# Moving key counts from a routing stage to the experts, with smaller last routing chunks and the first expert's rows read in pieces

## The chip, the cores and the metric

The kernel runs on one core of one Trainium2 chip. The metric is device time in microseconds of one execution; a median of several executions is compared. All data is float32, and everything from the input `x` to the output is one launch.

The core has five engines, each with a queue of its own that is worked off in order: TensorE (PE in the profile; its weight loads are PEld), VectorE (DVE), ScalarE (ACT), GpSimd (POOL) and SyncE (SP). Transfers are issued from SP's, ACT's or POOL's queue and run on 16 DMA engines.

## The reference, cut to what matters

The reference is a network of two layers on `x` of shape (2, 1024, 256), so 2048 tokens of 256 values. Each layer is an adapter, an attention, another adapter and a feed-forward part:

```python
x = x + L0_attn(L0_cond(x))      # adapter, then an RWKV-like recurrence
x = x + L0_ffn(L0_cond2(x))      # two-layer adapter (256 -> 1024 -> 256), then 8 experts, top 2
x = x + L1_attn(L1_cond(x))      # dense or sparse attention, then local attention
x = x + L1_ffn(L1_cond2(x))
```

The change lies in the second line and at the start of the third. The experts' part takes the two largest of eight gate logits of each token, keeps at most 512 tokens an expert in the order of arrival (first all first choices, then all second choices), and adds up the weighted results:

```python
for k in range(TOP_K):
    oh = jax.nn.one_hot(idx[:, k], E, dtype=jnp.int32)
    pos = jnp.cumsum(oh, axis=0) - 1 + counts[None, :]
    keep = (oh == 1) & (pos < CAPACITY)
    counts = counts + jnp.sum(keep.astype(jnp.int32), axis=0)
    combine = combine + w[:, k][:, None] * keep.astype(jnp.float32)
for e in range(E):
    h = jax.nn.gelu(xf @ W1[e] + b1[e])
    ye = h @ W2[e] + b2[e]
    out = out + combine[:, e][:, None].astype(xf.dtype) * ye
```

The sparse form of `L1_cond` lets each of 1024 queries attend to 32 listed keys, whose numbers lie between 0 and 255 and can occur more than once. A softmax over a list with repeats is a softmax over all keys, with the logarithm of each key's count added to its score. The kernel computes it so.

## The kernel before, in words

Activations are kept transposed, as tiles of 128 channels by tokens, in blocks of 128 tokens. There are 16 blocks.

**cond2 and routing.** `cond2_0` works through the chunks of `C2CK` (line 607): three of four blocks, one of three, one of one. For each chunk TensorE multiplies by the first weights into `ph` (L629), ScalarE applies Gelu (L632), TensorE multiplies by the second weights into `po` (L638), once for each half `c` of the 256 channels, and VectorE adds the bias into `c2` (L645). Then `choose(ch)` computes the gate logits `pl` (L723), copies them to `L` (L727), transposes the tokens (L657) into rows `ct` (ScalarE, L729), and finds the two largest logits by a chain of small dependent VectorE operations (L735 to L745). `place(ch)` turns the choices `oh` into running counts by matmuls into `pc` (L758, L762), into slots (L767 to L778, the last being `si`), and scatters the rows into the DRAM table `xs` by indirect DMAs from POOL's queue (L781), two for each block. `place` of a chunk is issued one chunk later; the last two come at the end. `finish` computes the weights of the combination and the number of first choices of each expert.

**Experts.** `moe` loops over eight experts. SP loads the expert's 512 rows by first choice (`xe`) and by second choice (`more`), 544 KB each (L919). VectorE merges them (L921), and computes the rows to which the results go (`row`, L927 to L931). TensorE transposes (L936), ScalarE copies (`xt`, L937), TensorE multiplies into `ph` (L942), ScalarE applies Gelu into `h` (L945, two buffers), TensorE multiplies into `po` (L950, two buffers), VectorE adds the bias (`ye`, L953), POOL scatters to `ys` (L954). Weights of the expert after next are loaded by SP (L892, L894). Each expert is followed in the program by `count_keys`, which for one block of 128 queries compares the 256 key numbers `iok` with each of the 32 listed keys and adds up: 1 operation (L879) and 31 steps (L881) that depend on each other, then a mask for zero counts, a maximum with 1, a logarithm on ScalarE and a sum (L883 to L886). The result is `lc`.

**After the experts.** `combine` loads the results from `ys` by SP's and ACT's queues (L974), weights and adds them (L978, L979), transposes and adds into `x` (L981, L984). Then come the projections of `L1_cond` (L1046 and on) and its attention, whose first operation on the scores reads `lc` (L1164).

**What sets the order.** The program is written in the order above, but the instructions of each engine are ordered at compile time by a scheduler that fills an engine with later work when earlier work is not ready. Waits follow from the tiles that an instruction reads, writes or takes over. So `count_keys`, which depends only on small inputs loaded by `load_counts` (L860, L862) ahead of cond2, stands in VectorE's queue between the operations of cond2, far ahead of its place in the program. Tiles come from pools on the left or right side of the on-chip memory; a tile that takes over another's space waits for that tile's last user.

Of the kernel before, what the change touches and what calls it, by code (L numbers as in the profile page):

```python
# [9 lines left out]
F32 = mybir.dt.float32  # L10
I32 = mybir.dt.int32
U8 = mybir.dt.uint8
AF = mybir.ActivationFunctionType
# [5 lines left out]
P = 128  # L19
# [584 lines left out]

C2CK = [(0, 4), (4, 4), (8, 4), (12, 3), (15, 1)]


def cond2_0(k, x, o, choose, place):  # L610


    nc, tc = k.nc, k.tc
    with (
        tiles(tc, name="c2s", bufs=2) as sp,
        tiles(tc, name="c2p", bufs=3, space=PSUM) as pp,
        tiles(tc, name="c2q", bufs=2, space=PSUM) as qp,
    ):

        end = len(C2CK) - 1  # L620
        for ch, (b0, nb) in enumerate(C2CK):
            b = b0 * P // S
            n = nb * P
            ts = slice(b0 * P, b0 * P + n)
            h = sp.tile([P, 8, CK], F32, name="h")
            for m in range(8):
                ph = pp.tile([P, CK], F32, name="ph")
                for c in range(2):
                    nc.tensor.matmul(  # L629
                        ph[:, 0:n], lhsT=k.c2w1[:, c, m * P : (m + 1) * P], rhs=x[:, c, ts], start=c == 0, stop=c == 1  # L630
                    )
                nc.scalar.activation(h[:, m, 0:n], ph[:, 0:n], AF.Gelu, bias=k.vec("c2b1", m))  # L632
            if 0 < ch < end:
                place(ch - 1)
            for c in range(2):
                po = qp.tile([P, CK], F32, name="po")
                for m in range(8):
                    nc.tensor.matmul(  # L638
                        po[:, 0:n],
                        lhsT=k.c2w2[b][:, m, c * P : (c + 1) * P],  # L640
                        rhs=h[:, m, 0:n],
                        start=m == 0,
                        stop=m == 7,
                    )
                nc.vector.tensor_scalar_add(o[:, c, ts], po[:, 0:n], k.c2b2[b][:, c : c + 1])  # L645
            if ch == end:
                place(ch - 1)
            choose(ch)
        place(end)

# [200 lines left out]
            nc.vector.tensor_mul(k.cw[:, kk, :], val[kk], self.kept[:, :, kk])  # L851


def load_counts(k, pool):

    nc, ins = k.nc, k.ins
    k.idx = pool.tile([P, 8, 32], F32, name="idx")
    with tiles(k.tc, name="ldc", bufs=1) as lp:
        ii = lp.tile([P, 8, 32], I32, name="ii")
        nc.sync.dma_start(out=ii, in_=ins["idx"].rearrange("(q p) j -> p q j", p=P))  # L860
        mm = lp.tile([P, 8, 32], U8, name="mm")
        nc.sync.dma_start(out=mm, in_=ins["idxm"].rearrange("(q p) j -> p q j", p=P))  # L862
        mf = lp.tile([P, 8, 32], F32, name="mf")
        nc.vector.tensor_copy(mf, mm)
        nc.vector.tensor_copy(k.idx, ii)

        nc.vector.scalar_tensor_tensor(k.idx, k.idx, 1.0, mf, ALU.add, ALU.mult)
        nc.vector.tensor_scalar_add(k.idx, k.idx, -1.0)
    k.lc = pool.tile([P, 8, NEAR], F32, name="lc")
    k.iok = pool.tile([P, S], F32, name="iok")  # L870
    nc.gpsimd.iota(k.iok, pattern=[[1, S]], base=0, channel_multiplier=0, allow_small_or_imprecise_dtypes=True)


def count_keys(k, sp, n, qb):


    nc = k.nc
    key = k.iok[:, 0 : n.shape[-1]]
    nc.vector.tensor_scalar(n, key, k.idx[:, qb, 0:1], None, ALU.is_equal)  # L879
    for j in range(1, 32):  # L880
        nc.vector.scalar_tensor_tensor(n, key, k.idx[:, qb, j : j + 1], n, ALU.is_equal, ALU.add)  # L881
    none = sp.tile([P, n.shape[-1]], F32, name="none")
    nc.vector.tensor_scalar(none, n, 0.0, -BIG, ALU.is_equal, ALU.mult)  # L883
    nc.vector.tensor_scalar_max(n, n, 1.0)
    nc.scalar.activation(n, n, AF.Ln)
    nc.vector.tensor_add(n, n, none)  # L886


def load_expert(k, wp, e):
# [8 lines left out]
def moe(k, xs, ys, wp, loaded):  # L898


    nc, tc, ins = k.nc, k.tc, k.ins
    with (
        tiles(tc, name="mos", bufs=2) as sp,
        tiles(tc, name="moc", bufs=1) as cp,
        tiles(tc, name="mop", bufs=2, space=PSUM) as pp,
    ):
        b2 = cp.tile([P, E * C], F32, name="b2")
        nc.sync.dma_start(out=b2, in_=ins["mb2"].to_broadcast([P, E * C]))
        rows = dram_disjoint_views(ys[:], E * 4)

        own = cp.tile([P, E, 4], F32, name="own")
        nc.gpsimd.iota(
            own, pattern=[[CAP, E], [P, 4]], base=2 * T, channel_multiplier=1, allow_small_or_imprecise_dtypes=True
        )
        for e in range(E):
            w1, w2 = loaded[e]
            xe, more = (sp.tile([P, 4, ROW], F32, name=n) for n in ("xe", "more"))
            for t, r0 in ((xe, e * CAP), (more, NSLOT + e * CAP)):
                nc.sync.dma_start(out=t, in_=xs[r0 : r0 + CAP, :].rearrange("(j p) f -> p j f", p=P))  # L919
            for j in range(4):  # L920
                nc.vector.scalar_tensor_tensor(  # L921
                    xe[:, j, :], more[:, j, :], k.more[:, e, j : j + 1], xe[:, j, :], ALU.mult, ALU.add
                )

            no = xe[:, :, C]
            empty = sp.tile([P, 4], F32, name="empty")
            nc.vector.scalar_tensor_tensor(empty, no, 0.0, own[:, e], ALU.is_equal, ALU.mult)  # L927
            to = sp.tile([P, 4], F32, name="to")
            nc.vector.scalar_tensor_tensor(to, k.more[:, e], float(T), no, ALU.mult, ALU.add)
            row = sp.tile([P, 4], I32, name="row")  # L930
            nc.vector.scalar_tensor_tensor(row, to, -1.0, empty, ALU.add, ALU.add)  # L931
            xt = sp.tile([P, 2, CAP], F32, name="xt")
            for c in range(2):
                pt = pp.tile([P, CAP], F32, name="pt")
                for j in range(4):
                    nc.tensor.transpose(pt[:, j * P : (j + 1) * P], xe[:, j, c * P : (c + 1) * P], k.ident)  # L936
                nc.scalar.copy(xt[:, c, :], pt)  # L937
            h = sp.tile([P, 8, CAP], F32, name="h")
            for m in range(8):
                ph = pp.tile([P, CAP], F32, name="ph")  # L940
                for c in range(2):
                    nc.tensor.matmul(  # L942
                        ph, lhsT=w1[:, c, m * P : (m + 1) * P], rhs=xt[:, c, :], start=c == 0, stop=c == 1
                    )
                nc.scalar.activation(h[:, m, :], ph, AF.Gelu_apprx_tanh, bias=k.vec("mb1", e * 8 + m))  # L945
            ye = sp.tile([P, 4, C], F32, name="ye")
            for j in range(4):
                po = pp.tile([P, C], F32, name="po")
                for m in range(8):
                    nc.tensor.matmul(  # L950
                        po, lhsT=h[:, m, j * P : (j + 1) * P], rhs=w2[:, m, :], start=m == 0, stop=m == 7
                    )
                nc.vector.tensor_add(ye[:, j, :], po, b2[:, e * C : (e + 1) * C])  # L953
                nc.gpsimd.indirect_dma_start(  # L954
                    out=rows[e * 4 + j],
                    out_offset=bass.IndirectOffsetOnAxis(ap=row[:, j : j + 1], axis=0),
                    in_=ye[:, j, :],
                    in_offset=None,
                )
            if e + 2 < E:  # L960
                loaded.append(load_expert(k, wp, e + 2))
            count_keys(k, cp, k.lc[:, e, :], e)


def combine(k, x, ys):
# [20 lines left out]

def load_cond1(k, pool):
    nc, ins = k.nc, k.ins
    k.w1c = pool.tile([P, NW1C], F32, name="w1c")

    k.bk = pool.tile([P, 4], F32, name="bk")
# [276 lines left out]
def cond1_heads(k, b, qT, kT, v, aT, sp, pp, tp):  # L1268
# [6 lines left out]
    def scores(it):  # L1275
        qb, h0 = it["at"]
        if h0 == 0:
            mk8 = sp.tile([P, S], U8, name="mk8")
            nc.sync.dma_start(out=mk8, in_=ins["mask"][qb * P : (qb + 1) * P, :])
            mk = sp.tile([P, S], F32, name="mk", bufs=1)  # L1280
            nc.vector.tensor_scalar_add(mk, mk8, -1.0)
            t = state["bias", qb] = sp.tile([P, S], F32, name="bias")
            count_keys(k, sp, t, qb)
            nc.vector.tensor_scalar_mul(t, t, k.sel[:, b : b + 1])
            nc.vector.scalar_tensor_tensor(t, mk, k.coef[:, b : b + 1], t, ALU.mult, ALU.add)
        ps = [pp.tile([P, S], F32, name=f"ps{i}", bufs=1) for i in range(2)]
# [416 lines left out]
def program(ctx: ExitStack, tc: tile.TileContext, ins, out):  # L1703
# [40 lines left out]
    with tiles(tc, name="c", bufs=1) as cp, tiles(tc, name="w3k", bufs=1, side="right") as kp:  # L1744
        c2 = cp.tile([P, 2, T], F32, name="c2")
        with tiles(tc, name="cnt", bufs=1) as np_:
            with tiles(tc, name="mor", bufs=1, side="right") as rp:
                with tiles(tc, name="mow", bufs=2, side="right") as ep:
                    with tiles(tc, name="mort", bufs=1, side="right") as rt:
                        with (  # L1750
# [1 line left out]
                            tiles(tc, name="rtp", bufs=1, space=PSUM) as pp,  # L1752
                        ):
                            load_cond2_0(k, wp)
                            load_counts(k, np_)
                            load_cond1(k, np_)
                            loaded = [load_expert(k, ep, e) for e in range(2)]
                            route = Route(k, c2, xs, rp, rt, pp, pp)
# [121 lines left out]
```

## Time and profile before

| what | us |
|---|---|
| median of 3 runs | 1566.27 (1561.85 to 1575.56) |
| profiled execution | 1573.28 |
| its span, first to last instruction | 1571.6 |
| PE busy | 1453.8 (93%) |
| DVE busy | 876.0 (56%) |
| ACT busy | 686.1 (44%) |
| POOL busy | 186.6 (12%) |
| key count steps L881, 248 of them | 103.7 on DVE, between 302.9 and 438.4 |
| cond2 and routing on PE | 300.1 to 426.4 |
| experts on PE | 445.4 to 680 |

A line of the costliest groups gives line, engine, operation, output and inputs with shapes and count, then the busy time and the mean duration in ns, then the idle time of the engine ahead of them with what ended it. A line of the timeline gives the start, the duration, the engine, the line of the kernel and the operation, with the idle time of the engine ahead of it in brackets. The "queue" lines (SPq) are issues of transfers. The clock column is the TensorE clock that was granted, as a share of full speed. A float32 matmul shows as two records, so 16 records make one `po` tile of an expert.

### The profile page before, as it was taken

The page shows a single profiled execution, that of the slowest core. Times are in us where ns is not written, and L with a number is a line of the kernel's source. Part 1 is how long each engine was busy: PE and PEld are TensorE (multiplying, and loading weights), DVE is VectorE, ACT ScalarE, POOL GpSimd, SP SyncE. Part 2 cuts the span into 40 slices and gives each one's busy share as a digit, 9 for nine tenths or more (in the row PEclk, how much of TensorE's full clock was granted, in tenths as well). Part 3 has the DMA queues.
Part 4 walks back from the last instruction along what each step waited for, and adds up shares of the span by engine and source line. Part 5 has one row for each costly group of instructions (what it writes and reads, how often), then busy time and mean ns, then how long its engine had stood idle before and what let it go on. Part 6 is the DMA issues. An engine that isn't in the chain of part 4 may idle for free. (4 is left out here: it accounts for less than half of the span.)

```text
span 1571.6 us, 27458 instructions
## 1 busy us (share of the span) xinstructions
PE 1453.8 (93%) x10842; PEld 994.2 (63%) x10842; DVE 876.0 (56%) x2791; ACT 686.1 (44%) x1675; POOL 186.6 (12%) x167
## 2 busy tenths in 40 slices
PE   5998779999869999979999989999999999999897
PEld 2445768544646676655666634778886478888765
DVE  3544663599931111055888711788782167878454
ACT  2433013333421212204988821667574265656543
POOL 1532430014411011010000010000000000000021
PEclk8899678999979999987999999999999999999999
DMA  9500003401153333030000020000000000000001
GB/s 301 176 1 2 3 3 112 161 4 40 53 162 132 124 115 115 14 120 1 2 2 2 2 82 0 1 2 2 1 2 1 0 1 2 2 1 2 1 19 36
DMA packets 42631, 70.79 MB, mean 45 GB/s; under 512 B 7040, under 2 KB 35712, under 8 KB 39424
## 3 DMA queue, kind: packets, MB, share of 16 engines
q1 hardware_dynamic: 36224, 56.11, 10.7%
q0 software_dynamic: 3072, 8.65, 1.5%
q10 hardware_dynamic: 3200, 4.19, 0.8%
q8 instruction: 88, 1.44, 0.4%
q14 instruction: 47, 0.39, 0.1%
HBM read 45.09 MB, written 23.86 MB: 44 GB/s over the span
## 5 line engine op out<-in xcount | busy, mean ns | idle before, releaser
L1543 ACT ACTIVATE pe<-pe,nm 128x320 f32<-128x320 f32 x256 | 141.9, 555 | 133.3 <-DVE nm L1533 133.1
L1533 DVE CUSTOM_DVE_ANT_0 pe<-ps,wbs 128x320 f32<-128x320 f32 x256 | 118.7, 487 | 5.9 <-PE ps L1527 2.5
L1174 ACT ACTIVATE pe<-pe,nm 128x256 f32<-128x256 f32 x256 | 110.6, 498 | 22.1 <-DVE nm L1164 22.1
L942 PE MATMUL ph<-xt,w 128*128 128x512 f32 x256 | 114.2, 604 | 2.0 <-ACT xt L937 2.0
L1523 PE MATMUL ps<-kT,qT 64*128 64x384 f32 (+1 forms) x512 | 109.2, 498 | 3.3 <-DVE qT L1497 2.8
L950 PE MATMUL po<-w,h 128*128 128x256 f32 x512 | 111.8, 379 | 0.0
L950 PEld LDWEIGHTS po<-w,h 128*128 128x128 f32 x512 | 97.3, 190 | 16.6 <-issue 3.8
L1164 DVE CUSTOM_DVE_ANT_0 pe<-ps,lc 128x256 f32<-128x256 f32 x256 | 94.0, 417 | 19.7 <-PE ps L1148 19.7
L953 DVE TENSOR_TENSOR ye<-po,b 128x256 f32<-128x256 f32 x32 | 13.6, 425 | 163.8 <-PE po L950 163.8
L881 DVE SCALAR_TENSOR_TENSOR lc<-iok,idx,lc 128x256 f32<-128x256 f32 x248 | 103.7, 476 | 0.0
L1592 PE MATMUL py<-ptt,v 128*64 128x128 f32 x1408 | 102.3, 277 | 0.1
L942 PEld LDWEIGHTS ph<-xt,w 128*128 128x128 f32 x256 | 48.6, 193 | 62.2 <-issue 55.8
L1592 PEld LDWEIGHTS py<-ptt,v 128*64 128x64 f32 x1408 | 78.2, 137 | 10.5 <-issue 7.6
L1183 PE MATMUL ptp<-ident,pe 128*128 128x128 f32 x512 | 76.8, 291 | 5.8 <-ACT pe L1174 3.2
L1565 PE MATMUL pt<-ident,pe 128*128 128x128 f32 x512 | 79.0, 281 | 1.8 <-DVE pe L1551 0.7
L1183 PEld LDWEIGHTS ptp<-ident,pe 128*128 128x128 f32 x512 | 57.6, 146 | 35.6 <-ACT pe L1174 21.2
L945 ACT ACTIVATE h<-ph,vecs 128x512 f32<-128x512 f32 x64 | 44.0, 687 | 70.7 <-PE ph L942 70.7
L1552 ACT ACTIVATE pe<-pe,rd 128x320 f32<-128x320 f32 x128 | 70.7, 558 | 5.7 <-DVE rd L1550 5.6
L1527 PEld LDWEIGHTS ps<-sk,qT 64*128 64x128 f32 x512 | 50.7, 187 | 26.0
L1427 PE MATMUL pq<-c,w1ak 128*128 128x512 f32 x128 | 61.3, 623 | 5.6 <-ACTq L1765 5.6
L1572 DVE TENSOR_TENSOR ptt<-pt,tri 128x512 f32<-128x512 f32 x96 | 64.9, 676 | 0.0
L1565 PEld LDWEIGHTS pt<-ident,pe 128*128 128x128 f32 x512 | 56.2, 141 | 9.9 <-ACT pe L1552 1.3
(339 smaller groups left out, 2828.2 us busy)
## 6 DMA issues: line engine op xcount, KB each, us to landing
w<-in_mw SPq DMA_DIRECT2D x16, 1024.0 KB, 5.0
xs<-z SPq DMA_DIRECT2D x8, 1088.0 KB, 11.7
xe<-xs SPq DMA_DIRECT2D x8, 544.0 KB, 6.0
more<-xs SPq DMA_DIRECT2D x8, 544.0 KB, 4.0
ys<-z SPq DMA_DIRECT2D x4, 1024.0 KB, 11.4
x<-in_xT ACTq DMA_DIRECT2D x4, 512.0 KB, 5.8
g<-ys SPq DMA_DIRECT2D x4, 512.0 KB, 9.6
g<-ys ACTq DMA_DIRECT2D x4, 512.0 KB, 10.9
```

The costliest lines, as they stand in the source:

```text
L881: nc.vector.scalar_tensor_tensor(n, key, k.idx[:, qb, j : j + 1], n, ALU.is_equal, ALU.add)
L942: nc.tensor.matmul(ph, lhsT=w1[:, c, m * P : (m + 1) * P], rhs=xt[:, c, :], start=c == 0, stop=c == 1)
L950: nc.tensor.matmul(po, lhsT=h[:, m, j * P : (j + 1) * P], rhs=w2[:, m, :], start=m == 0, stop=m == 7)
L1164: nc.vector.tensor_tensor_reduce(out=pe[:, j, :], in0=it["ps"][i][:, j, :], in1=k.lc[:, q0 + j, :], scale=-1.0, scalar=3.0e38, op0=ALU.add ...
L1174: nc.scalar.activation(pe[:, j, :], pe[:, j, :], AF.Exp, bias=nm, scale=-1.0)
L1183: nc.tensor.transpose(ptp[:, kb, j, :], it["pe"][i][:, j, kb * P : (kb + 1) * P], k.ident)
L1523: nc.tensor.matmul(ps[:, i, keys[i]], lhsT=qs[i], rhs=kT[hp, m + pair, k0 : k0 + nk], start=True, stop=True)
L1533: nc.vector.tensor_tensor_reduce(out=pe[:, i], in0=ps[:, i, used[i]], in1=wbs[:, 0 if n == 0 else 3 if n == NB - 1 else 1 + i, (1 - i) * G ...
L1543: nc.scalar.activation(pe[:, i], pe[:, i], AF.Exp, bias=nm[:, i : i + 1], scale=-1.0, accum_out=den[:, i : i + 1])
L1552: nc.scalar.activation(pe[:, 1], pe[:, 1], AF.Copy, scale=rd[:, 1:2])
L1565: nc.tensor.transpose(pt[1 - j if i and inner(n) else j][:, 2 * pair + i, :], pe[:, at : at + P], k.ident)
L1592: nc.tensor.matmul(py[64 * i : 64 * i + 64, (m + pair) % 4, :], lhsT=keys[:, hs], rhs=it["pts"][:, pair, :] if j == 3 else it["pt"][:, j, ...
```

## The change

Five edits:

- **Chunks.** The last chunks of `C2CK` are 2, 1 and 1 blocks instead of 3 and 1. In the last chunk the `place` of the chunk before it stands after the first half `c = 0` of the second projection, no longer after both.
- **Count inputs.** `load_counts` (two small loads and four VectorE operations) is called inside `moe`, after the first expert's row loads. Its scratch lies on the right side, where the routing tiles lay. The tiles `idx`, `lc` and `iok` and the filling of `iok` move to `load_cond1`.
- **Counts.** `count_keys` keeps only the comparisons.
- **Logarithm.** A new function `log_counts` does mask, maximum, logarithm and sum; it is called once after the eight experts, on all of `lc`, 2048 columns, with the sum on GpSimd. Its two scratch tiles are named `h` and share the two buffers of the experts' `h`. In the branch for lists with far keys it follows `count_keys` directly.
- **Rows of the first expert.** For `e == 0` each of the two loads is cut into four of 136 KB, `xe` on SP's queue and `more` on ACT's.

```diff
-C2CK = [(0, 4), (4, 4), (8, 4), (12, 3), (15, 1)]
+C2CK = [(0, 4), (4, 4), (8, 4), (12, 2), (14, 1), (15, 1)]
...
                 nc.vector.tensor_scalar_add(o[:, c, ts], po[:, 0:n], k.c2b2[b][:, c : c + 1])
-            if ch == end:
-                place(ch - 1)
+                if ch == end and c == 0:
+                    place(ch - 1)
             choose(ch)
...
-def load_counts(k, pool):
+def load_counts(k):
     nc, ins = k.nc, k.ins
-    k.idx = pool.tile([P, 8, 32], F32, name="idx")
-    with tiles(k.tc, name="ldc", bufs=1) as lp:
+    with tiles(k.tc, name="ldc", bufs=1, side="right") as lp:
...
-    none = sp.tile([P, n.shape[-1]], F32, name="none")
+
+
+def log_counts(k, eng, n, none, ln):
+
+    nc = k.nc
     nc.vector.tensor_scalar(none, n, 0.0, -BIG, ALU.is_equal, ALU.mult)
     nc.vector.tensor_scalar_max(n, n, 1.0)
-    nc.scalar.activation(n, n, AF.Ln)
-    nc.vector.tensor_add(n, n, none)
+    nc.scalar.activation(ln, n, AF.Ln)
+    eng.tensor_add(n, ln, none)
...
-            for t, r0 in ((xe, e * CAP), (more, NSLOT + e * CAP)):
-                nc.sync.dma_start(out=t, in_=xs[r0 : r0 + CAP, :].rearrange("(j p) f -> p j f", p=P))
+            pieces = [slice(j, j + 1) for j in range(4)] if e == 0 else [slice(0, 4)]
+            for js in pieces:
+                for t, r0, queue in ((xe, e * CAP, nc.sync), (more, NSLOT + e * CAP, nc.scalar if e == 0 else nc.sync)):
+                    src = xs[r0 : r0 + CAP, :].rearrange("(j p) f -> p j f", p=P)
+                    queue.dma_start(out=t[:, js], in_=src[:, js])
+            if e == 0:
+                load_counts(k)
...
-            count_keys(k, cp, k.lc[:, e, :], e)
+            count_keys(k, k.lc[:, e, :], e)
+
+        log_counts(k, nc.gpsimd, k.lc, *(sp.tile([P, 8, NEAR], F32, name="h") for _ in range(2)))
...
                             load_cond2_0(k, wp)
-                            load_counts(k, np_)
                             load_cond1(k, np_)
```

More of the change, by code (lines that the diff above doesn't have):

```diff
@@ L868, in load_counts, with count_keys @@
         nc.vector.tensor_scalar_add(k.idx, k.idx, -1.0)
[L869 to L874, printed above, removed]
+def count_keys(k, n, qb):
     nc = k.nc
@@ L988, in load_cond1 @@
     nc, ins = k.nc, k.ins
+    k.idx = pool.tile([P, 8, 32], F32, name="idx")
+    k.lc = pool.tile([P, 8, NEAR], F32, name="lc")
+    k.iok = pool.tile([P, S], F32, name="iok")
+    nc.gpsimd.iota(k.iok, pattern=[[1, S]], base=0, channel_multiplier=0, allow_small_or_imprecise_dtypes=True)
     k.w1c = pool.tile([P, NW1C], F32, name="w1c")
@@ L1282, in scores @@
             t = state["bias", qb] = sp.tile([P, S], F32, name="bias")
-            count_keys(k, sp, t, qb)
+            count_keys(k, t, qb)
+            log_counts(k, nc.vector, t, *(sp.tile([P, S], F32, name=n, bufs=1) for n in ("none", "ln")))
             nc.vector.tensor_scalar_mul(t, t, k.sel[:, b : b + 1])
```

## The prediction

> **What bounds the kernel now.** I read the page first, for the engine that sets the pace and for the slices where it rests.
>
> ```profile
> PE   5998779999869999979999989999999999999897
> ...
> DVE  3544663599931111055888711788782167878454
> ...
> L881 DVE SCALAR_TENSOR_TENSOR lc<-iok,idx,lc 128x256 f32<-128x256 f32 x248 | 103.7, 476 | 0.0
> ```
>
> Each digit is a tenth of busy time in a slice of 39.3 us. TensorE is full nearly everywhere; the change touches slices 8 to 18, and there only slices 11 and 12 (393 to 471 us) fall to 8 and 6. VectorE is full in slices 9 to 11, where the key counts (L881) run, and at 1 in the seven slices of the experts. Next, busy time by stretch around that hole (busy us of PE, PEld, DVE, ACT, POOL, then clock, DMA share, GB/s):
>
> ```profile
> 420.00:426.40 6.40, 6.40 (x60) 6.39 (x58) 5.88 (x27) 1.73 (x5) 1.14 (x1) 1.00 0.12 44
> 426.40:445.40 19.00, 1.78 (x8) 1.45 (x7) 13.26 (x79) 4.08 (x6) 7.71 (x8) 0.54 0.44 145
> 445.40:451.55 6.15, 5.90 (x13) 2.97 (x14) 3.68 (x13) 2.36 (x3) 0.00 (x0) 0.50 0.96 285
> 451.55:480.00 28.45, 28.45 (x105) 18.88 (x104) 3.68 (x10) 6.56 (x10) 3.83 (x4) 0.99 0.30 94
> ```
>
> TensorE rests 19 us between cond2 and the first expert, then works at half clock to 451.55. Before and after it is 100% busy. So the prize is this hole and nothing else; the timeline says what fills it:
>
> ```profile
> 426.80 0.15 DVE L727 COPY L<-pl 128x8 f32<-128x8 f32 x1
> 431.33 0.15 DVE L742 TENSOR_TENSOR oh<-cand,first 128x8 f32<-128x8 f32 x1
> 433.56 0.15 DVE L778 TENSOR_TENSOR si<-q,at 128x2 int32<-128x2 f32 x1
> 435.41 1.00 POOL L781 DMA_INDIRECT xs<-ct,si  x1 [0.30 <-issue]
> 436.71 0.96 POOL L781 DMA_INDIRECT xs<-ct,si  x1 [0.30 <-issue]
> 439.29 0.38 SPq L919 DMA_DIRECT2D xe<-xs  x1
> 444.80 1.74 DVE L921 SCALAR_TENSOR_TENSOR xe<-more,xe 128x272 f32<-128x272 f32 x4 [4.30 <-DMA more<-xs]
> 447.77 5.75 PE L942 MATMUL ph<-xt,w 128*128 128x512 f32 x8 [0.25 <-ACT xt L937]
> ```
>
> A serial chain: the last block's logits are copied, top-2 chosen, slots computed, two scatters queued, rows read back once all scatters landed, merged, transposed, multiplied. Last, the waits inside the experts, and the two scatters by tile:
>
> ```profile
> DVE ye L953 <- PE po L950: 163.8, 32, 18.2
> DVE row L931 <- DMA ys<-ye,row: 37.8, 6, 6.6
> ```
> ```profile
> L781 POOL DMA_INDIRECT xs<-ct,si x32: 954/1154/4053, 348.3 to 436.7; - x32
> ```
> ```profile
> L954 POOL DMA_INDIRECT ys<-ye,row x32: 955/959/962, 468.4 to 680.8; - x32
> ```
>
> VectorE waits for TensorE beside the experts, never the reverse; but it also stands 6.6 us in `row` (L931) for a scatter to land.
>
> **What the Trainium skill says.** "SBUF — State Buffer", section "Who interferes with whom": a VectorE instruction with two SBUF inputs contends with a GpSimd one that reads SBUF, under an exclusive lock. The trace agrees in direction: scatters beside counts take 1154 ns at the median and up to 4053, those beside an idle VectorE 955 to 962. "ScalarE: Activation LUTs", "What ACT_TABLE_LOAD costs": about 1283 ns per switch of table set; the trace shows 1283. "DMA: Bandwidth & Descriptors", "Issuing engines are not separate DMA queues": a second queue saves only issue time. The trace agrees so far: from 442 to 447 us one queue already moved 342 to 384 GB/s at a DMA share over 1.0. "TensorE: Matmul & The Clock Gate", "What's actually happening": after idleness the clock is halved until a window of some 3.4 us was busy; here it stayed at 0.50 for 3.8 us after the first expert matmul.
>
> **The change, part by part.**
>
> *Counts leave cond2.* 256 steps that start 0.40 us apart (12 in 4.83 us) are 102 us of VectorE. In cond2 TensorE never waited for them (10.00 of 10 us busy from 370 to 420), so their leaving frees nothing there, save in the last chain: choose's 11 steps from 426.80 to 431.33 are 0.41 us apart because a count stands between them. Where none does, dependent steps are 0.20 to 0.23 apart (446.65 to 446.85, 433.05 to 433.28): 2.4 us instead of 4.5.
>
> *Chunks of 2, 1, 1.* A 3-block matmul pass takes 0.327 us, 2-block 0.216 (that of the experts' 256 columns), 1-block 0.117: 64 passes cost 64 x 0.006 = +0.4. `place` of block 14 now stands in front of the last 16 passes with 4 passes, +0.5, and the earlier `place`, 0.8 of which ran after the last projection, also stands ahead. End of projections: 425.12 + 0.4 + 0.5 + 0.8 = 426.8. Evacuation and gate matmuls: +1.4 (425.12 to 426.5, the copy at 426.80 being held by `place`): copy at 428.2. Choose 2.4 and its last operation 0.15: 430.8. `place`: matmuls at half clock 1.0, vector steps 1.05 (432.66 to 433.71), hand-over to POOL 0.7: 433.6. POOL is then free: six of the eight scatters that queued from 427.83 on went out earlier. Before, this backlog delayed the last pair by 1.0. Two scatters, 1.27 + 0.96: 435.8; landing and SP, 1.62 as before: reads start at 437.5 instead of 439.29, **-1.8**. TensorE could wait for `oh` of the earlier blocks, but 5.9 us of projection cover 2.7 of choose; were that cover gone, 1 us.
>
> *First rows in pieces.* Both loads are 1.09 MB, 2.9 us at some 370 GB/s, so the last piece lands no earlier, 5.5 after the first issue; this is a choice, bounded by 4.9 and 6.5. But merge, transpose and copy of earlier pieces run before it. After the last: merge 0.50, transpose 0.27, copy 0.59, hand-overs 0.3, 1.65 instead of 2.97: **-1.3**. The four `more` loads on ACT's queue, about 0.5 us issue each, stand before the `xt` copies, which come 6 us later: free; ACT waits there for the scatters with nothing else due.
>
> *load_counts moves* onto SP behind these pieces: issue 0.58 + 2.26 us. Behind it are expert 1's loads, now 3.5 us later relative to the first read. Their merge was done at 449.87, transposes due at 453.36: 3.5 us of cover, which this uses up. 0 to 1 us, taken **+0.3**. Its casts could be queued ahead of the last merge and hold the first expert for the small DMA (landing 4.2): up to +3, taken 0.
>
> *Counts beside the experts.* One expert is 29.0 us, VectorE's own part 3.9, so 25 us of counts fit and four experts carry them. A late `ye` matters once it is 2.8 us late (a `po` tile takes 3.45 us, the add 0.42, two buffers). Taken **+0.3**; the other end is the first rival.
>
> *Logarithm once.* Gone from ACT: 8 x (0.42 + 2 x 1.28) = 24 us, which lay beside full TensorE: 0. New, at the end: two vector passes of at most 2.3 us, one Ln (1.06 at 1024 columns, so some 1.9 at 2048), a POOL add (2.2 at 1024, so 4.4). Their scratch takes `h`'s two slots, so Ln cannot start before the last expert matmul (680); add over by 687, while the next vector work on `combine` begins at 688.50 and `lc` is first read at 723.34. **0**; with POOL holding the lock longer, up to +4.
>
> Sum: -1.8 - 1.3 + 0.3 + 0.3 = **-2.5 us**. The profiled execution took 1573.28 (span 1571.6 and 1.7 around it), so 1570.8 of its kind; it was 0.4% above the median of 1566.27. Against that median: **1563.8**.
>
> **Rivals.** *Counts stall TensorE (slower than before).* Queues are in order, their order fixed in advance. `row` waits 6.5 us after an expert's last `ye` (478.53 to 485.01). Counts queued behind it wait too, and with VectorE otherwise full it reaches the next `ye` late by what was blocked. From 2.8 on, TensorE pays: with under 9 counts (3.7 us) queued ahead of `row`. With four ahead: 6.5 - 1.6 - 2.8 = 2.1 per expert, four experts, 8.4; minus 2.8: 1572. With none, and scatters starved by the lock, 15 to 25 us. For it: the 37.8 us wait and the 4053 ns scatter; against: in cond2 the same filler reached each evacuation within 0.1 us of TensorE's end.
>
> *The hole stays.* The chain is shorter but the small-packet count loads or the read-back end last: 1566. For it: DMA share over 1.0 in the read-back; against: the pieces precede the count loads in program order.
>
> *More comes.* Earlier transposes also end the half clock earlier (it cost 1.9 us), and scatters land sooner: 1560. Against: the clock's window asks for sustained work.
>
> **How the numbers follow.** Forecast 0.57 (1563.8, 1561 to 1566), stall 0.25, hole stays 0.11, more 0.07. About 1% (15.7 us) is what a measurement of this kernel can tell from no change; the three runs alone lie 0.9% apart. The hole is only 21 us, so faster by over 1%: 0.04. Slower by over 1% is the stall near its upper end: 0.07. The range, 1556 to 1574, takes in the stall's middle and the spread of the runs, and leaves out its upper end.
>
> **What would show it.** Reads of `xe` starting some 11 us after the last cond2 matmul; choose steps 0.2 apart; first L942 within 7.2 us of the first read; L881 between 445 and about 570 us; one Ln; TensorE still 100% busy between experts, with no wait of L950 on `ye`. I am wrong if L950 waits for L953, if the first L942 follows the count loads, or if `combine` starts later after the last expert.

## The result, and the profile after

The kernel before takes 1568.32 us (median, beside the changed one), the changed kernel **1583.04 us**: the ratio is 1.0092, with a 95% interval of 1.0071 to 1.0112, so 14.5 us slower (11 to 18) where 2.5 us faster was forecast. The profiled execution of the changed kernel took 1577.85 us (span 1576.1).

The two profiles differ by less than that, 4.6 us, because what stands ahead of cond2 had a mean clock of 0.87 in the changed kernel's profile and of 0.85 in the other, and took 6.5 us less. So from here on a stage is timed from its own start. Line numbers after the change are 1 higher in `cond2_0` and `choose`, and 5 higher in `moe` (`row` L936, `po` L955, `ye` L958); `g` is loaded in L981, `log_counts` stands in L883 to L886. "To first matmul" is from cond2's first matmul to the first expert's first L947, which is cond2 and the hole together. The last column is the same kernel on another chip; it belongs to the experiments and stands here so that the table need not be repeated.

| stage, us | before | predicted step | changed | changed, other chip |
|---|---|---|---|---|
| cond2, first matmul to last token transpose | 126.5 | +1.7 | 134.5 | 126.1 |
| hole, from there to the first expert matmul | 21.2 | -4.8 | 16.7 | 16.7 |
| to first matmul (the two rows above) | 147.6 | -3.1 | 151.1 | 142.8 |
| experts, first matmul to last `ye` | 232.7 | +0.6 | 241.8 | 242.9 |
| last `ye` to the combine's first vector step | 8.0 | 0 | 13.0 | 13.3 |
| from there to the first projection | 4.8 | 0 | 4.1 | 4.1 |
| projections and attention of `L1_cond` | 207.9 | 0 | 204.1 | 204.0 |
| sum against before | | -2.5 | +13.0 | +6.1 |
| measured against before | | | +14.5 | +6.9 (3.4 to 10.2) |

The changed kernel's stretches (busy us of PE, PEld, DVE, ACT, POOL, then clock, DMA share, GB/s) show cond2 first.

```profile
400.00:403.90 3.90, 3.89 (x30) 3.51 (x28) 0.69 (x3) 0.37 (x1) 2.92 (x4) 1.00 0.30 107
403.90:408.40 4.50, 1.61 (x11) 1.24 (x11) 2.23 (x13) 1.18 (x4) 1.92 (x2) 0.92 0.25 93
408.40:417.70 9.30, 9.30 (x43) 9.30 (x44) 1.36 (x10) 1.82 (x6) 2.83 (x3) 0.50 0.09 30
```

At block 14, the new one-block chunk, TensorE rests for 2.9 of 4.5 us (these rests are called bubbles below) and then works for 9.3 us at half clock, which costs some 4.7 more: together 7.6 of the 8.0 us. Next, the chain of the experts: from the waits (engine, line, what ended the wait: total, times, longest) and the timeline.

```profile
DVE row L936 <- DMA ys<-ye,row: 27.4, 6, 6.4
...
PE po L955 <- DVE ye L958: 6.0, 3, 2.7
```
```profile
482.45 0.16 DVE L936 SCALAR_TENSOR_TENSOR row<-to,empty 128x4 int32<-128x4 f32 x1 [4.24 <-DMA ys<-ye,row]
...
489.47 8.79 DVE L877 SCALAR_TENSOR_TENSOR lc<-iok,idx,lc 128x256 f32<-128x256 f32 x22
...
498.18 0.42 DVE L958 TENSOR_TENSOR ye<-po,b 128x256 f32<-128x256 f32 x1
...
498.65 1.83 PE L955 MATMUL po<-w,h 128*128 128x256 f32 x6 [1.96 <-DVE ye L958]
```

VectorE stands 4.24 us in `row`, works through its counts, and reaches `ye` at 498.18; TensorE, with both `po` buffers full, waits 1.96 us. Before, no `po` waited for `ye`. Last, the end of the experts.

```profile
689.40 4.49 POOL L886 TENSOR_TENSOR lc<-h 128x2048 f32<-128x2048 f32 x1 [1.66 <-ACT h L885]
...
689.42 2.14 ACTq L981 DMA_DIRECT2D g<-ys  x4
...
693.92 2.03 SPq L981 DMA_DIRECT2D g<-ys  x4
...
699.50 0.62 DVE L985 TENSOR_SCALAR o<-g,cw 128x256 f32<-128x256 f32 x2 [11.50 <-DMA g<-ys]
```

SP's half of the `g` loads starts when GpSimd's add ends (689.40 + 4.49 = 693.89), though the add has nothing to do with `g`.

### The profile page after: what moved, and what is told of

Read it like the earlier page. It is cut to its first block, busy times and chain, and to the rows that moved or that the text cites. A ratio compares the mean times of both kernels' runs of the same rounds, so it can differ in the third digit from the quotient of the medians.

```text
span 1576.1 us, 27608 instructions
## 1 busy us (share of the span) xinstructions
PE 1448.9 (92%) x10908; PEld 997.8 (63%) x10908; DVE 879.9 (56%) x2797; ACT 672.6 (43%) x1664; POOL 179.0 (11%) x168
## 5 line engine op out<-in xcount | busy, mean ns | idle before, releaser
L955 PE MATMUL po<-w,h 128*128 128x256 f32 x512 | 114.4, 384 | 6.0 <-DVE ye L958 6.0
L947 PE MATMUL ph<-xt,w 128*128 128x512 f32 x256 | 114.1, 603 | 2.7 <-ACT xt L942 2.7
L955 PEld LDWEIGHTS po<-w,h 128*128 128x128 f32 x512 | 98.0, 192 | 24.5 <-DVE ye L958 7.5
L1175 DVE CUSTOM_DVE_ANT_0 pe<-ps,lc 128x256 f32<-128x256 f32 x256 | 94.0, 418 | 21.2 <-PE ps L1159 21.2
L947 PEld LDWEIGHTS ph<-xt,w 128*128 128x128 f32 x256 | 48.7, 193 | 62.8 <-issue 55.9
L950 ACT ACTIVATE h<-ph,vecs 128x512 f32<-128x512 f32 x64 | 44.0, 688 | 71.4 <-PE ph L947 71.4
L630 PE MATMUL ph<-x,c2w 128*128 128x512 f32 (+2 forms) x192 | 60.7, 462 | 1.3 <-ACT h L633 0.8
```

The lines of the kernel that those rows point to most:

```text
L947: nc.tensor.matmul(ph, lhsT=w1[:, c, m * P : (m + 1) * P], rhs=xt[:, c, :], start=c == 0, stop=c == 1)
L955: nc.tensor.matmul(po, lhsT=h[:, m, j * P : (j + 1) * P], rhs=w2[:, m, :], start=m == 0, stop=m == 7)
L1175: nc.vector.tensor_tensor_reduce(out=pe[:, j, :], in0=it["ps"][i][:, j, :], in1=k.lc[:, q0 + j, :], scale=-1.0, scalar=3.0e38, op0=ALU.add ...
```

## The experiments

**Three costs, three repairs.** The first four kernels ran on one chip. The first gives the logarithm a scratch of its own.

```diff
-        log_counts(k, nc.gpsimd, k.lc, *(sp.tile([P, 8, NEAR], F32, name="h") for _ in range(2)))
+        with tiles(tc, name="lgs", bufs=1, side="right") as lg:
+            log_counts(k, nc.gpsimd, k.lc, *(lg.tile([P, 8, NEAR], F32, name=n) for n in ("none", "ln")))
```

> The changed kernel with the logarithm's two scratch tiles in memory of their own, on the other side of SBUF, where no tile of the combine lies. Theory (memory handed on): SyncE's g loads no longer wait for GpSimd's add, so the first vector step of the combine starts about 8.5 us after the last ye instead of 13.4; 4.5 us less than the changed kernel, ratio to the kernel before 1.0063. Rival (the logarithm's own work, or GpSimd's lock, is what costs): the g loads start as late as before or the combine's vector work is slowed by as much, ratio 1.009. Since the scratch no longer waits for the last expert, the logarithm moves ahead to where the counts end; its two table loads and one Ln, 4.5 us of ScalarE, could hold TensorE by 1 to 3 us there, in which case the gain is 2 to 3 us. The bubbles of the first one-block chunk (1.6, 0.55 and 0.75 us without a matmul, then half clock to 418) are expected again if they belong to the program, absent if they were chance in one execution.

Measured 1.0126 (1.0086 to 1.0166), slower still. The wait did go: the combine's first step comes 9.0 us after the last `ye`. But the scheduler now put the logarithm among the experts, between two of their Gelus:

```profile
577.73 1.28 ACT L885 ACT_TABLE_LOAD   x1 [2.50 <-issue]
...
579.02 1.91 ACT L885 ACTIVATE ln<-lc 128x2048 f32<-128x2048 f32 x1
...
580.95 1.28 ACT L950 ACT_TABLE_LOAD   x1
...
582.99 9.54 PE L947 MATMUL ph<-xt,w 128*128 128x512 f32 x15 [3.62 <-ACT h L950]
```

1.28 + 1.91 + 1.28 us of ScalarE stop TensorE for 3.62 us, and that expert takes 35.2 us instead of 29.0, at a mean clock of 0.90. In cond2 eight smaller logarithms had cost little: with the new chunks and the counts there it takes 128.0 us with them (f3_before_chunks_pieces, below) and 126.3 without (h4_counts_in_cond2_log_late, on another chip). Beside an expert's `ph` one costs more. The bubbles of cond2 were there again (132.4 us).

The second kernel moves the counts back beside cond2.

```diff
                             load_cond1(k, np_)
+                            load_counts(k)
...
-            if e == 0:
-                load_counts(k)
```

> The changed kernel with load_counts called ahead of cond2, as in the kernel before, so that the counts run beside cond2 again; chunks, pieces and the single logarithm at the end are kept. Theory (counts stall the experts): no wait of a po matmul on ye is left, expert periods are 29.0 us again instead of 30.6 to 32.9, and 9 us of the changed kernel's loss go; but choose's steps are 0.41 us apart again, which gives back some 1.8 of the hole. Sum 14.5 - 9 + 1.8 = +7.3 us, ratio 1.0047. Rival (the experts are longer for the clock, not for the waits): periods stay near 30 us and the ratio stays at 1.008 or more.

Measured 0.9992 (0.9968 to 1.0016). Experts 232.3 us, no `po` waits for `ye`; the hole is 18.7 us. The ratio is below the 1.0047 of the theory because, unexpectedly, cond2 takes 126.9 us, without a bubble, on a chip where two other kernels with the same chunks have them. The third takes the chunks back.

```diff
-C2CK = [(0, 4), (4, 4), (8, 4), (12, 2), (14, 1), (15, 1)]
+C2CK = [(0, 4), (4, 4), (8, 4), (12, 3), (15, 1)]
...
-                if ch == end and c == 0:
-                    place(ch - 1)
+            if ch == end:
+                place(ch - 1)
```

> The changed kernel with the last chunks of 3 and 1 blocks and the old place of place(14). Theory (the one-block chunk in the middle starves ScalarE and TensorE of each other and drops the clock): cond2 takes 126 to 127 us from its first to its last matmul instead of 134.4, ratio 1.0092 - 0.005 = 1.004, less up to 1 us for a longer choose. Rival (the bubbles were chance in one execution, or come from the counts' absence): cond2 is as long as in the other kernels that keep the 2, 1, 1 split, and the ratio stays at 1.008 to 1.009.

Measured 1.0051 (1.0029 to 1.0073); cond2 126.1 us, the hole 20.2, experts 241.3. So on this chip the bubbles came only with both: the one-block chunk, and a cond2 without the counts. The fourth gives each expert its own `row`.

```diff
-            row = sp.tile([P, 4], I32, name="row")
+            row = cp.tile([P, 4], I32, name=f"row{e}")
```

> The changed kernel with a row tile for each expert, so that row is never held until the scatters of the expert two before have landed; nothing else is changed. Theory (the wait for the scatter blocks VectorE's queue, and the counts behind it reach ye late): the waits of po matmuls on ye (6.0 us in all) go, the expert periods with counts fall from 30.6 to 32.9 to 29.0 to 29.5, 7 to 9 us less than the changed kernel, ratio 1.0035 to 1.005. Rival (the counts are too many for the order they stand in: 22 to 31 in a row ahead of a ye): the waits on ye stay at 4 to 6 us in all with no wait in row, ratio 1.008 to 1.009.

Measured 1.0023 (1.0004 to 1.0042). The waits on `ye` are gone, and three experts in a row, with all their counts, read (columns as above):

```profile
482.07:511.05 28.98, 28.69 (x104) 19.09 (x104) 28.98 (x80) 6.58 (x11) 3.84 (x4) 1.00 0.46 151
511.05:540.03 28.98, 28.69 (x104) 19.09 (x104) 28.98 (x78) 6.57 (x11) 3.83 (x4) 1.00 0.39 129
540.03:569.01 28.98, 28.69 (x104) 19.10 (x104) 28.36 (x73) 6.57 (x11) 5.81 (x4) 1.00 0.38 130
```

VectorE is busy all 28.98 of 28.98 us in two of them, and TensorE keeps the pace of before. That decides between the two explanations: not how many counts there are, but the one instruction in their queue that waits for a transfer.

**Repairs together.** The next four ran on another chip. The first has the row tiles and the logarithm behind the first `g` loads.

```diff
-        log_counts(k, nc.gpsimd, k.lc, *(sp.tile([P, 8, NEAR], F32, name="h") for _ in range(2)))
...
                 queue.dma_start(out=g[kk], in_=ys[r0 : r0 + CK, :].rearrange("(j p) f -> p j f", p=P))
+            if b4 == 0:
+                with tiles(tc, name="lgs", bufs=1, side="right") as lg:
+                    log_counts(k, nc.gpsimd, k.lc, *(lg.tile([P, 8, NEAR], F32, name=n) for n in ("none", "ln")))
```

> The row tiles of the run before, and the logarithm moved into the combine, behind the first g loads, its scratch in the memory of the experts' weights. In e1_scratch the scratch was free early and the logarithm went in among the experts, so that run did not test the end alone; this one does. Theory (the g loads wait for the add because they take over the scratch's memory): the first vector step of the combine comes about 8.5 us after the last ye instead of 13.2, 4.5 us less than with the row tiles alone, ratio 0.9995. Rival (GpSimd's add, 4.5 us, and the two vector passes cost the combine as much wherever they stand, by the order of VectorE's queue or the shared lock): 13 us again or longer o steps, ratio 1.002.

Measured 0.9919 (0.9892 to 0.9945, from six runs), lower than the 0.9995 of the theory: the end falls only to 10.1 us where 8.5 were forecast, but cond2 takes 126.1 us with no bubble, with the same instructions up to the combine as the run before. The second has the row tiles and, in `choose`, `nc.vector.tensor_copy` instead of `nc.scalar.copy` for `ct`.

> The row tiles, and the token copies ct of choose made by VectorE, which without the counts has little to do in cond2. Theory (in a one-block chunk ScalarE is the engine that TensorE waits for: each h and ct comes late, and taking two or three copies away from it gives the slack back): the bubbles of the chunk of block 14 go or fall below 0.5 us, cond2 takes 126.5 to 128 us instead of 131 to 134, some 4 us less than with the row tiles alone, ratio 1.000. Rival (ScalarE starts late there for another reason, such as the scatters that run back to back at that time): its h steps are late as before, cond2 stays at 131 to 134 us, ratio 1.002 or more.

Measured 0.9989 (0.9971 to 1.0006), cond2 125.8 us. Since the run above shows no bubbles on this chip either, this tells nothing of ScalarE's part. The third is the kernel before with the new `C2CK`, the new `place` and the loads in pieces, edits as in the change.

> The kernel before with the chunks of 2, 1 and 1 blocks, the new place and the pieces on two queues alone; counts and their logarithms stay beside cond2. Theory (only the moves of the counts and of the logarithm cost, while the chunk split costs nothing where VectorE counts): no bubble at block 14, experts of 29.0 us, combine 8.0 us after the last ye; the hole is 1.3 us shorter for the pieces and 1 us for the chunks, ratio 0.998 to 0.999. Rival (the one-block chunk starves TensorE by itself): cond2 is 4 to 8 us longer, ratio 1.001 to 1.004.

Measured 0.9978 (0.9963 to 0.9992). Of its stages the hole is 2.5 us shorter (18.7) and cond2 1.5 longer (128.0). The fourth joins all three repairs.

> All three repairs on the changed kernel: row tiles, the logarithm behind the first g loads, ct on VectorE. If the three costs are separate they add up: from the changed kernel's 1.0092, 11 us for the row tiles as measured, 4.5 for the end, 4 to 8 for cond2: ratio 0.9945 to 0.9975, ahead of the kernel before. If they share one cause, or the combine pays for the logarithm wherever it stands, the ratio stays at 0.999 to 1.002.

Measured 0.9930 (0.9904 to 0.9956), a little below the forecast: not to be told from the first of these four.

**Is it the chip?** The next four ran on a third chip. The first is the changed kernel, unaltered.

> The changed kernel once more, unaltered, on the chip of the next three. The bubbles at the chunk of block 14 were there in three kernels (the changed one, e1_scratch, e4_row_tiles) and absent in f1_row_log_after_g, whose instructions are the same up to the combine. Theory (they come and go by the execution or the chip, not by the program): this execution shows cond2 at 126 us or at 131 to 134 us without regard to the program, and the one below agrees with it if the chip decides. Rival (the program decides): cond2 131 to 134 us again. Ratio 1.006 to 1.009 in both.

Measured **1.0044** (1.0022 to 1.0065), with cond2 at 126.1 us. So the bubbles don't belong to the program alone. Nor do cond2's scatters explain them by themselves. Here are the stretches before and at the first bubble, first in the changed kernel's own profile, then here, at the same times after the start of cond2 (columns as above; what the DMA engines move here is nearly all rows of the scatters):

```profile
397.61:403.61 6.00, 6.00 (x40) 5.54 (x39) 0.97 (x2) 0.37 (x1) 4.59 (x5) 1.00 0.33 116
403.61:404.61 1.00, 0.28 (x3) 0.08 (x1) 0.82 (x5) 0.00 (x0) 0.69 (x2) 1.00 0.27 100
```
```profile
396.18:402.18 6.00, 6.00 (x41) 5.54 (x39) 1.42 (x5) 0.73 (x3) 4.59 (x5) 1.00 0.33 116
402.18:403.18 1.00, 1.00 (x11) 1.00 (x10) 0.83 (x6) 0.92 (x5) 0.70 (x2) 1.00 0.27 100
```

GpSimd is as busy and the same bytes move at the same time; only ScalarE differs, and then TensorE. At the first of the token copies, changed kernel and then here:

```profile
402.91 0.31 PE L658 MATMUL pt<-ident,c 128*128 128x128 f32 x1
...
405.06 0.37 ACT L730 COPY ct<-pt 128x256 f32<-128x256 f32 x1 [2.34 <-PE ph L630]
...
406.50 0.37 ACT L633 ACTIVATE h<-ph,vecs 128x128 f32<-128x128 f32 x1 [1.06 <-PE ph L630]
```
```profile
401.48 0.31 PE L658 MATMUL pt<-ident,c 128*128 128x128 f32 x1
...
401.82 0.37 ACT L730 COPY ct<-pt 128x256 f32<-128x256 f32 x1 [0.53 <-PE pt L658]
...
402.09 0.77 ACT L633 ACTIVATE h<-ph,vecs 128x128 f32<-128x128 f32 x2
```

The copy starts 2.15 us after the transpose instead of 0.34. Why ScalarE starts late is not settled; no trace shows what it waits for. The three profiles with bubbles come from the first comparison and from the chip of the first four kernels, where the kernels with the counts in cond2 or with the old chunks show none; the twelve on the three other chips show none either. As each group of four ran on one chip and at one time, the chip and the time can't be told apart. The next two are earlier kernels again, unaltered.

> The row tiles alone once more, on the same chip as the next. Its first measurement, 1.0023, was on another chip than f1_row_log_after_g, 0.9919, so that the 1% between them is not yet the logarithm's place. Theory (the place of the logarithm is worth what the stages show: 3.1 us to the combine's first vector step, and up to 2 more behind it): 0.995 to 0.9985 here if the bubbles are absent. Rival (the whole 1% belongs to the logarithm's place): 1.001 to 1.003 with cond2 at 126 us.

Measured 0.9956 (0.9926 to 0.9987): 14 us below the changed kernel on the same chip by the ratios, 11 by the medians, where the experts explain 9.0 (234.0 against 242.9) and a higher clock in the attention of `L1_cond` another 3.8 (171.9 against 175.7).

> The row tiles and the logarithm behind the first g loads once more, for a narrower interval (its first had six runs). Theory: 0.990 to 0.995 where cond2 shows no bubbles, 0.994 to 0.998 where it does. Rival (the first measurement was chance): 0.997 to 1.000 with cond2 at 126 us.

Measured 0.9961 (0.9939 to 0.9982), cond2 126.1 us, the end 9.7: between the theory and the rival, so the first measurement was in part chance or its chip. The 1% between e4_row_tiles and f1_row_log_after_g is not the logarithm's place: on one chip that place, worth 3.2 us to the combine's first step and 2.3 to the first projection, does not show above the spread. The row tiles alone gained 0.0067 between the two chips, some 10 us, of which cond2 is 5.0 and the attention's clock 3.4. The fourth has the old chunks beside both repairs (the edits of f1 and of e3).

> The same with the last chunks of 3 and 1 blocks and the old place: what the chunk split alone is worth when the counts are out of cond2. Theory (the split shortens the hole, by 3.3 us in the stages of e3_old_chunks against the changed kernel): 3 us longer than the run above where that one shows no bubbles, 1 to 5 us shorter where it does. Rival (cond2's end is reached as late with both splits): the same time.

Measured 0.9961 (0.9940 to 0.9981), the same as g3. Its hole is 21.2 us against 17.0, its cond2 125.4 against 126.1, so it is 3.5 us longer to the first matmul, which the interval cannot resolve.

**What the end costs alone.** The last four ran on a fourth chip, which shows no bubbles. First the logarithm moved as in f1, without the row tiles.

> The changed kernel with the logarithm behind the first g loads alone; row is shared as in the changed kernel. Theory (the end is a cost of its own): the waits of po on ye stay at 6 us and the experts at 242 us, while the combine's first vector step comes 9.7 to 10.1 us after the last ye instead of 13.0 to 13.3; 3 us less than the changed kernel on a chip of the same kind: 1.0025 where cond2 takes 126 us, 1.007 where it takes 131 to 134 us. Rival (the gain of f1_row_log_after_g came from the row tiles and the chip alone): 1.0044 and 1.0092.

Measured 1.0001 (0.9975 to 1.0027): experts 242.9 us, the end 10.2. The wait for memory is a cost of its own, 3 us, of which 1.0 is given back before the first projection. What is left of the end stands in g3's timeline:

```profile
676.00 1.22 DVE L883 TENSOR_SCALAR none<-lc 128x2048 f32<-128x2048 f32 x1
...
676.36 2.23 POOL L959 DMA_INDIRECT ys<-ye,row  x1 [2.50 <-DVE ye L958]
...
680.12 2.47 SPq L980 DMA_DIRECT2D g<-ys  x4
```

The last scatter, beside the logarithm's vector passes, takes 2.23 us instead of 0.96, and the loads that read its result start that much later. The next kernel therefore puts the logarithm after the combine's vector work, in two halves.

```diff
+        for q in range(0, 8, 4):
+            log_counts(k, nc.gpsimd, k.lc[:, q : q + 4], *(gp.tile([P, 4, C], F32, name=f"g{kk}", bufs=4) for kk in range(2)))
```

> The row tiles, and the logarithm after the combine's vector work, in two halves whose scratch is that of g. In g3_row_log_again two vector passes of 1.22 us lay beside the last scatter, which took 2.23 us instead of 0.96, and the first vector step of the combine stayed 1.7 us behind the kernel before. Theory (that is VectorE against GpSimd at the last scatter): 8.0 to 8.3 us after the last ye again, 1.5 us less than g3, ratio 0.995. Rival (ScalarE's Ln, 3.4 us with its table, now between evacuations of kT, holds TensorE): up to 3 us more, ratio 0.997 to 0.998. With cond2 at 131 to 134 us both are 0.0035 higher.

Measured 0.9967 (0.9948 to 0.9986). The end is 8.3 us again and the last scatter takes 0.96, so it was VectorE against GpSimd. But the gain is paid back at once:

```profile
705.78 0.69 DVE L883 TENSOR_SCALAR g<-lc 128x1024 f32<-128x1024 f32 x1
...
706.38 0.75 DVE L1067 TENSOR_SCALAR qT<-pq,vecs 128x512 f32<-128x512 f32 x1
...
707.18 5.29 PE L1058 MATMUL pq<-x,w1c 128*128 128x256 f32 x9 [3.13 <-DVE qT L1067]
```

The projections wait 3.13 us for `qT`, which stands in VectorE's queue behind the passes. The rival had named ScalarE's Ln for this; it was VectorE. The last two add `ct` on VectorE, and put the counts back beside cond2 (edits as above; the last keeps the shared `row`, which without counts behind it holds nothing up).

> The same with ct on VectorE. Only a chip that shows the bubbles at the chunk of block 14 tells anything here; f2_row_ct_vector ran on one that does not show them in other kernels either. Theory (ScalarE's late starts meet a chunk in which it is the engine waited for): where the run above has cond2 at 131 to 134 us, this one has 126 to 128 us. Rival (late starts, whatever ScalarE has to do): 131 to 134 us in both. Where the run above has 126 us, both kernels take the same time within 2 us.

> The counts beside cond2 again, with the chunks, the pieces and the logarithm after the combine's vector work: whether the counts' move among the experts is worth anything once its costs are repaired. Theory (the move shortens only choose's last chain): hole 18.7 us instead of 16.7 to 16.9, all else equal, 1.8 us slower than h2_row_log_late where that one's cond2 takes 126 us, and some 4 us faster where it takes 131 to 134 us. Rival (the counts also hold back scatters and evacuations in cond2): 4 us or more slower than h2 with cond2 at 128 us or more.

Measured 0.9969 (0.9950 to 0.9987) and 0.9971 (0.9952 to 0.9990). Without bubbles the first tells nothing of them. The second says that, with its costs repaired, the move of the counts is worth nothing that can be measured: without it the hole is 2.0 us longer (19.3 against 17.3), but the whole to the first projection only 0.4 us.

Nine of these last twelve measurements lie below the kernel before with their whole interval, all by less than 1%, two of them (f3 and h4) with the counts still beside cond2. The lowest are f1 and f4, at 0.9919 and 0.9930; f1 again, as g3, is at 0.9961. To the first projection the profiles of f1 and g3 are only 0.2 and 1.4 us ahead of the kernel before; 7.8 us each are the clock of the attention (last section).

## Why the prediction was wrong, step by step

**To the first matmul** (predicted -3.1): right in mechanism, too small, where the chip adds nothing: -4.8 (142.8 against 147.6). The hole came out nearly as worked out, 4.5 us shorter where 4.8 follows from the sum: choose's steps are 0.20 apart (428.13, 428.32), and the first read starts 9.2 us after the last token transpose instead of 12.7. What was mis-sized is cond2, +1.7 in the sum and -0.3 there. The split costs 0.7 (126.1 in g3 against 125.4 in g4), and the counts and logarithms, whose leaving was to free nothing ahead of the last chain, gave back 1.1 (125.4 against 126.5). Nor is choose's shorter chain worth anything by itself. In g4, without counts but with the old chunks, the hole is 21.2 us as before:

```profile
426.43 0.23 DVE L743 TENSOR_TENSOR oh<-cand,first 128x8 f32<-128x8 f32 x1
...
434.09 0.96 POOL L782 DMA_INDIRECT xs<-ct,si  x1 [0.30 <-issue]
...
436.65 1.75 SPq L922 DMA_DIRECT2D xe<-xs  x4
```

Its last `oh` comes 2.5 us after the last transpose instead of 4.7, but the eight scatters go out back to back and the last one at 10.1 us, as before. The split alone (f3) gains 2.5 us of hole, the two together 4.5.

In the compared execution cond2 added 8.0 us: the step that priced the smaller chunks at +0.4 for their passes didn't ask how late ScalarE may be when a block's `ph` takes TensorE some 0.5 us instead of 1.3 (4 records of 0.117 or 0.327). That this is why its lateness shows there is argued from the places of the bubbles, not shown. The cover that I did price, 1 us for `oh`, was another one and wasn't needed.

**"Counts beside the experts, +0.3"** is the step that failed on every chip that ran it: +9.1 in the compared execution, +10.2 in g1, +8.6 and +10.2 in e3 and h1. The first rival had the mechanism to the letter, `row` holding the counts behind it and these holding `ye`. It priced 2.1 us for each of four experts; measured are three waits of 1.30 to 2.71 us, 6.0 in all, and with them TensorE at 0.95 of its clock in one expert (30.64 busy us instead of 29.00). Its upper end, scatters starved by VectorE, did not come: the 15 scatters that ran beside counts took 961 to 962 ns, though in cond2 of the kernel before 6 of 28 had taken over 1300, and in e4 one of 15 took 2936. I held the rival at 0.25 because in cond2 the same filler reached each evacuation in time. But nothing in VectorE's queue there waits for a transfer, so that this was no evidence for a queue that holds `row`, and the profile before already showed `row` standing for 6.6 us. That wait was harmless only while nothing stood behind it.

**"Logarithm once, 0"** failed too: +5.0 and +5.3. I compared the add's end with the first use of `lc` and with the combine's vector work, and named the memory that the scratch takes over. I did not ask who takes over the scratch: the `g` tiles do, and SP's loads inherit the wait. The 4 us that I kept as the other end belonged to a different mechanism, GpSimd's lock; the runs show a small form of it, 1.3 us at the last scatter of g3.

**Pieces**, predicted -1.3: from the first read to the first matmul it is 7.5 us in the changed kernel and 7.1 in g1, against 8.5 before, so -1.0 and -1.4. In g3 and g4 it is -0.5 and 0.0, because the last piece lands 6.3 and 6.5 us after the first read instead of 5.4: the upper bound that the prediction named was reached. **`load_counts`**: no fault found; its operations stand behind the last merge.

Of my three signs for being wrong two came true: L955 (L950 before) waits for `ye`, and the combine starts later. One reading of the page was loose: in the slices of the experts VectorE shows 1 in four, 0 in one, and 3 and 5 at the two ends. No term rests on it.

## What to carry to other kernels

Before free work is moved onto an engine's queue, look for every instruction there that waits for a transfer: its wait, harmless on an idle engine, becomes a delay for all that is queued behind it (6.0 us of TensorE here, none with the row tiles). For a scratch tile ask not only whose memory it takes but who takes its memory next, since that tile's loads wait for the scratch's last user. Work that hides in one stage (a logarithm in cond2, where ScalarE is busy for 49 of 126 us) is not free in another, even one where ScalarE has less to do (6.6 of 29.0 us beside an expert).

## What was not expected of the hardware

- **ScalarE can start late for no reason that a trace shows.** At the one-block chunks (blocks 14 and 15) single instructions of ScalarE started 0.5 to 2.5 us after the matmuls that they read and the instruction before them had ended, in the changed kernel, e1 and e4. On the three other chips no start in cond2 was more than 0.4 us late. The changed kernel costs 1.0092 in the first case and 1.0044 in the second.
- **Bubbles of 1.6, 0.55 and 0.75 us were enough to halve TensorE's clock for 9.3 us.** In e1 bubbles of 0.77 and 2.15 us halved it for 3.4 us; in e4 similar ones, the longest 1.44 us, did not. The Trainium skill, "TensorE: Matmul & The Clock Gate", section "What's actually happening", says that the monitor's window runs freely, which would let the same gaps be judged differently; the runs fit that and don't prove it.
- **A VectorE pass with one SBUF input slowed a scatter**, from 0.96 to 2.23 us in g3, and to 2.23 or 2.24 in each of the twelve traces where a scatter starts during such a pass of 2048 columns. "SBUF — State Buffer", "Who interferes with whom", has `tensor_scalar` among those that can take the port pair shared with GpSimd; the trace agrees.
- **The attention of `L1_cond` runs at several paces.** From the first score to the last transpose it takes 171.8 to 171.9 us at clock 1.00 in f1, g2, g3 and h2, 179.6 at 0.95 in the kernel before, 175.8 and 175.7 at 0.97 in the changed one, and for the row tiles alone 175.4 at 0.97 in e4 but 171.9 at 1.00 in g2. Most of what the profiles of f1 and g3 gain over the one profile of the kernel before lies here, not at the hole. Why the clock differs stays open.
